# Attention's output turned by VectorE and transfers within SBUF, with statistics, additions and ends put in another order

## The chip, the cores and the metric

One core of a Trainium2 chip runs the kernel. The metric is device time in microseconds (us) for one launch, the median of several runs. Engines: TensorE (PE; its weight loads are PEld), VectorE (DVE), ScalarE (ACT), GpSimd (POOL), SyncE (SP, which here only issues transfers). Each engine works through its own instructions in the order of the program, and engines wait for each other by semaphores.

## The reference, cut to what matters

Two layers over 32 graphs of 512 nodes with 512 features, all float32. `adj` is one 512 x 512 matrix of zeros and ones for all graphs.

```python
q, k, v = (x @ W + b for W, b in ...)                 # 8 heads of 64
scores = einsum('bihd,bjhd->bhij', q, k) / sqrt(64) + where(adj == 0, -1e9, 0)
out = einsum('bhij,bjhd->bihd', softmax(scores), v)   # layer 0: attention
x = layernorm(x + out)
x = layernorm(x + einsum('nm,bmd->bnd', adj, x) @ weight + bias)   # layer 1
```

## The kernel before

One batch `b` is one graph. A tile holds 128 partitions; the 512 rows of `x` lie as four blocks in `X[b]` (names `xs`, in the last batch `xT`). All work is written out by hand in one order (`manual_schedule`), and a batch is a loop step in which the stages of neighbouring batches are laced together: while batch `b` does attention, PE also makes q, k and v of batch `b+1` and layer 1 of batch `b-1`.

Products of 512 x 512 are done in seven block products of 256 x 256 instead of eight (the Winograd form of Strassen's method): `project` for q, k, v and `convolve` for layer 1's second product, each 8 matmul records on PE for one product (L367). The order in `convolve` is 1, 2, 5, 6, 7, 3, 4. Product 1 is copied by ScalarE into `MIX` (L533). VectorE adds products 6 and 7 to `MIX` (L535) and GpSimd adds `MIX` to the blocks x12, and x22 and x21 (L537). VectorE adds the others straight from the bank (L539).

Attention works on heads in pairs (`hp`, 2 x 64 = 128 partitions) and pairs in groups of two (`g`; two groups per batch):

- `scores` (L563): keys x queries into PSUM banks. VectorE takes each bank out with the mask added (L565), ScalarE takes the exponential (L567), GpSimd adds the four exponentials of a pair over the key blocks (L578, `es`).
- `attend` (L587): values x exponentials, so that the output comes as 128 head features x 512 nodes. ScalarE copies it out of its bank into `attT` (L591).
- `fold_squares`: VectorE turns `es` in 32 x 32 squares (L598) and sums (L600); `add_up` has PE finish the sums (L608), VectorE inverts them (`inverse`).
- `residual`: PE turns `attT` back into rows (L619, against the identity), VectorE multiplies by `inverse` (L622) and adds to `X[b]` (L624).

Then come the row statistics (`statistics`, VectorE, L429 and L430), square root and normalisation (ScalarE, L433 and L444), the split of the rows into a high and a low part[...] (`split_high` on ScalarE, L455; `split_low` on VectorE, L459, followed by the bias addition on GpSimd, L460), `aggregate` (L486: adjacency times both parts) and `convolve`.

PSUM has eight banks, handed out in turn by `bank()`: a matmul that needs a bank waits until what was in it eight banks earlier has been taken out. `units_of(b)` lists the interleaved work of a batch in order, and `work_until` runs a share of it at each point:

```python
        for hp in range(g * PAIRS, (g + 1) * PAIRS):
            attend(b, hp)
        folded = folds(b, g)
        ...
        later = scores(*groups[i + 1])
        add_up(b, g)
        ...
        work_until((0.6 if b != B - 2 else 1.0) if g else 0.85)
        for hp in range(g * PAIRS, (g + 1) * PAIRS):
            residual(b, hp)
        work_until(1.0)
```

So PE sees, per batch: attention of group 0, scores of group 1, products of q, k and v, residual, attention of group 1, scores of the next batch's group 0, v's remaining products and `aggregate`, residual, `convolve`. All transfers go through SP's queue: `load_squares` (L248, 16 issues per batch, x in pieces of 128 bytes for the next q, k, v), and `turn_over`: the store of batch `b-2` (L470) and the load of batch `b` (L233) into the same buffer.

After the last batch a tail finishes layer 1 of the last two batches. There `judge` checks that a fast path's conditions held; if not, a general kernel, not run here, would do the work again.

Of the kernel before, what the change touches and what calls it, by code (L numbers as in the profile page):

```python
# [37 lines left out]
FP = mybir.dt.float32  # L38
# [9 lines left out]
P = 128  # L48
HD = 64
# [9 lines left out]
SQ = 32  # L59
# [148 lines left out]
def fast_kernel(ctx: ExitStack, tc, verdict, x, adj, Wq, bq, Wk, bk, Wv, bv, W1, b1, out):  # L208
# [14 lines left out]
    def bank(*shape):  # L223

        return psum.tile([P, *shape], FP, name="bank", tag="bank", bufs=8)
# [56 lines left out]
        nc.gpsimd.tensor_add(fold, fold, ident[:, i * SQ:(i + 1) * SQ])  # L282
    eps = consts.tile([P, 1], FP, name="eps")
    nc.gpsimd.memset(eps, EPS)

    sums = consts.tile([P, NB, GROUP], FP, name="sums")
    inverses = consts.tile([P, NB, GROUP], FP, name="inverses")
# [237 lines left out]
    def convolve(b, i):  # L525

        pm = bank(2, half)
        block_product(pm, YT[b], w1, i)
        x11, x12, x21, x22 = (X[b][:, 2 * r:2 * r + 2, s * half:(s + 1) * half] for r in range(2) for s in range(2))
        if i == 1:  # L530

            MIX[b] = work.tile([P, 2, half], FP, name="mix", tag="q" if b >= B - 3 else "low", bufs=2)
            nc.scalar.activation(MIX[b], pm, AF.Copy)  # L533
        if i in (6, 7):
            nc.vector.tensor_add(MIX[b], pm, MIX[b])  # L535
            for block in (x12,) if i == 6 else (x22, x21):
                nc.gpsimd.tensor_add(block, block, MIX[b])  # L537
        for block in {1: (x11,), 5: (x12, x22), 2: (x11,), 3: (x12,), 4: (x21,)}.get(i, ()):
            nc.vector.tensor_add(block, pm, block)  # L539

    def aggregation(b):

# [4 lines left out]
        return [(convolve, b, i) for i in (1, 2, 5, 6, 7, 3, 4)] if b >= 0 else []  # L547


    E, ES, AT, SQUARES, PART, INVERSE = {}, {}, {}, {}, {}, {}  # L550
    PAIRS = GROUP // 2

    def scores(b, g):
# [26 lines left out]
    def attend(b, hp):  # L580
        po = bank(N)
        for j in range(NB):
            e = E.pop((b, hp, j))
            for s in range(2):
                h = 2 * (hp % 2) + s
                values = V[b][hp // 2][:, j, h * HD:(h + 1) * HD]
                nc.tensor.matmul(po[s * HD:(s + 1) * HD, :], values, e[:, s, :],  # L587
                                 start=(j == 0), stop=(j == NB - 1))
        SQUARES[b, hp] = work.tile([P, 2, N], FP, name="e", bufs=8)
        AT[b, hp] = work.tile([P, N], FP, name="attT")  # L590
        nc.scalar.activation(AT[b, hp], po, AF.Copy)  # L591

    def fold_squares(b, hp):

        if hp % PAIRS == 0:
            PART[b, hp // PAIRS] = work.tile([P, GROUP, N // SQ], FP, name="part", bufs=1)
        square = SQUARES.pop((b, hp))
        nc.vector.transpose(square.rearrange("p s n -> p (s n)"), ES.pop((b, hp)).rearrange("p s n -> p (s n)"))  # L598
        heads = slice(2 * (hp % PAIRS), 2 * (hp % PAIRS) + 2)
        nc.vector.tensor_reduce(PART[b, hp // PAIRS][:, heads, :], square.rearrange("p s (j f) -> p s j f", f=SQ),  # L600
                                axis=AX.X, op=ALU.add)
# [12 lines left out]

    def residual(b, hp):
        at = AT.pop((b, hp))
        pt = bank(NB, 2, HD)
        for c in range(NB):
            nc.tensor.transpose(pt[:, c, :, :], at[:, c * P:(c + 1) * P], ident)  # L619
        first = 2 * hp % GROUP  # L620
        inverse = INVERSE[b, 2 * hp // GROUP][:, :, first:first + 2]
        nc.vector.tensor_mul(pt, pt, inverse[:, :, :, None].to_broadcast([P, NB, 2, HD]))  # L622
        cols = X[b][:, :, hp * P:(hp + 1) * P]
        nc.vector.tensor_add(cols, pt.rearrange("p c s d -> p c (s d)"), cols)  # L624
        if hp == HP - 1 and b < B - 1:
            for c in range(NB):
                statistics(b, 0, c)

# [47 lines left out]
    def weighed(units):  # L676

        weight = {project: 0.5, aggregate: 0.55, x_transpose: 0.13, convolve: 0.5}
        return [(u, weight.get(u[0], 0.0)) for u in units]

    def units_of(b):

        made, turned = projections(b + 1), flips(b + 2)
        splits, gathered = aggregation(b - 1)
        young, old, seen = norm(b - 1, 0) if b < B - 1 else [], norm(b - 1, 1), survey(b - 2)
        ready = [(turn_over, b)] if 1 < b < B - 1 else []
        if b == B - 1:


            older = convolution(b - 2)  # L690
            lows = [(split_low, b - 1, d) for d in range(DB - 1)]
            units = weighed(lows[:2] + older[:3] + lows[2:] + splits[3:] + older[3:5] + older[5:] + gathered + seen)
            return units, [sum(w for _, w in units)] * 2

        if old:
            both = [[(f, b - 1, slice(0, 2 * NB))] for f in (square_root, invert_root)]
            behind = [seen[:2], seen[2:]] + both + [old[2:4], old[4:] + ready] + [[u] for u in young[2:]]
        else:
            behind = [ready] + [[u] for u in young]
        if b == 0:  # L700
            behind = [[]] + [[(sum_weights, w1, n)] for n in range(4)] + [[(look_for_low_half, c)] for c in range(NB)]
        behind += [[] for _ in range(11 - len(behind))] + [splits[:1], [], splits[1:2]]
        behind += [[] for _ in range(16 - len(behind))]
        units = []
        for k, unit in enumerate(made[:16]):
            units += [unit] + behind[k]
        first = sum(w for _, w in weighed(units))
        values = made[16:]
        units += values[:3] + gathered[:1] + splits[2:3] + gathered[1:2] + values[3:] + splits[3:]
        if b == B - 2 > 0:  # L710
            units += [(load, B - 1)]
        units += gathered[2:3] + turned[:1] + gathered[3:]
        convolved = convolution(b - 1) if b < B - 2 else []
        for k in range(7):
            units += convolved[k:k + 1] + (turned[k + 1:k + 2] if k < 3 else turned[4:] if k == 4 else [])
        units = weighed(units)
        return units, [first, sum(w for _, w in units)]

# [2 lines left out]
    for i, (b, g) in enumerate(groups):  # L721
        if g == 0:
            units, ends = units_of(b)
            done = 0.0

        def release():
            run(later)
            later.clear()

        def work_until(part):  # L730

            nonlocal done
            begin = ends[g - 1] if g else 0.0
            while units and (units[0][1] == 0 or done < begin + (ends[g] - begin) * part - 0.3):
                unit, w = units.pop(0)
                run([unit])
                done += w
                if unit[0] == (project if b < B - 1 else convolve):
                    if b == B - 1 or unit[3] == 7:
                        release()  # L740

        for hp in range(g * PAIRS, (g + 1) * PAIRS):
            attend(b, hp)
        folded = folds(b, g)
        if i == len(groups) - 1:
            run(folded)
            add_up(b, g)
            break
        run(folded[:1] + flips(1) + folded[1:] if i == 0 else folded)
        later = scores(*groups[i + 1])  # L750
        add_up(b, g)
        if g == 0 and b + 2 < B:
            load_squares(b + 2)
        work_until((0.6 if b != B - 2 else 1.0) if g else 0.85)
        for hp in range(g * PAIRS, (g + 1) * PAIRS):
            residual(b, hp)
        work_until(1.0)
        if g == GROUPS - 1:
            run([u for u, _ in units])
            if b == B - 2:  # L760
                run(norm(b, 0) + [(split_high, b, d) for d in range(DB - 1)])
        release()
# [17 lines left out]
    run(rest[3 + NB:])  # L780
    for c in range(NB):
        add_bias(t, c)
    run(seen[:2])
    aggregate_rows(t)


# [6 lines left out]
        nc.vector.bn_stats(halves[c][:, s, :], X[t][:, c, s * half:(s + 1) * half])  # L793

    old = norm(t, 1)
    beside = {1: seen[2:], 2: old[:2], 5: old[2:3], 6: old[3:5], 7: old[5:]}
    for unit in last:
        run([unit] + beside.get(unit[2], []))
        if unit[2] == 2:
            well = judge()  # L800
        if unit[2] == 7 and t > 0:
            store(t - 1)
        for c, s in {2: ((0, 0), (1, 0)), 3: ((2, 1), (3, 1), (0, 1), (1, 1)), 4: ((2, 0), (3, 0))}.get(unit[2], ()):
            half_statistics(c, s)
            if (c < 2) == (s == 1):
                if t + 1 not in STAT:
                    for table, name, shape in ((STAT, "stat", (2 * NB, 2)), (RSTD, "rstd", (2 * NB,)),
                                               (SHIFT, "shift", (2 * NB,))):
                        table[t + 1] = work.tile([P, *shape], FP, name=name, bufs=3)
                nc.vector.bn_aggr(STAT[t + 1][:, NB + c, :], halves[c])  # L810
# [35 lines left out]
```

## Time and profile before

| | |
|---|---|
| time, median of 3 runs | 2858.62 us (2857.77 to 2861.34) |
| span of the profile | 2858.2 us |
| PE busy | 2820.5 us (99%) |
| VectorE busy | 2086.4 us (73%) |
| GpSimd busy | 1746.2 us (61%) |
| ScalarE busy | 1146.6 us (40%) |
| granted TensorE clock | 0.996 |
| DMA, mean | 38 GB/s |

A share of busy time is an average over the whole span. The chain of work that ended last follows the waits back from the last instruction, and names at each moment the instruction that the end hung on. Columns in a row of the chain are start, length and what ran; in a row of the timeline start, length, engine, line, operation, output and inputs, and in brackets the idle time before it with what ended it. PE's rows count matmul records, of which one matmul instruction of this float32 kernel leaves two (the turning of `attT` and L486 leave one).

### The profile page before, as it was taken

To read this page: it belongs to the slowest core of one execution; us is meant where nothing else is said; L and a number is where in the kernel's file an instruction comes from. 1 tells how busy PE (TensorE), PEld (TensorE's weight loads), DVE (VectorE), ACT (ScalarE), POOL (GpSimd) and SP (SyncE) were. 2 spreads that over 40 slices of the span, in tenths; PEclk is the share of its full clock that TensorE was granted. 3 is DMA by queue.
4 is the path that set the end of the run, shared out by engine and by line. 5 is a ranking of instruction groups with operands and counts; after the bars stand their busy time and mean duration, and the time that the engine had idled before them with its cause. 6 is when DMAs were issued, how large, how long until landed. Compare 5 with 4: busy or idle time off the path is not lost.

```text
span 2858.2 us, 35612 instructions
## 1 busy us (share of the span) xinstructions
PE 2820.5 (99%) x13346; PEld 1983.1 (69%) x13346; DVE 2086.4 (73%) x3415; ACT 1146.6 (40%) x1550; POOL 1746.2 (61%) x1096
## 2 busy tenths in 40 slices
PE   8999999999999999999999999999999999999997
PEld 6676776766767767667677676676676766766765
DVE  6767777677776777777777767777677777777786
ACT  3344343343433443434434334343344342443443
POOL 4565665665756656656566656575665665665763
PEclk9999999999999999999999999999999999999998
DMA  5001111111101111011111111110111111111001
GB/s 154 12 8 41 45 30 30 41 34 45 45 16 45 34 41 45 16 45 34 41 45 35 25 42 33 45 45 15 45 34 41 45 24 36 36 39 45 30 16 45
DMA packets 302577, 108.81 MB, mean 38 GB/s; under 512 B 264256, under 2 KB 268352, under 8 KB 302400
## 3 DMA queue, kind: packets, MB, share of 16 engines
q1 hardware_dynamic: 302400, 106.47, 14.6%
q8 instruction: 108, 1.77, 0.3%
q14 instruction: 69, 0.57, 0.1%
HBM read 72.88 MB, written 33.55 MB: 37 GB/s over the span
## 4 chain that ended last, share of the span: by engine, by line
PE 96%; DVE 2%; POOL 1%; SPq 0%; issue 0%; ACT 0%; DMA 0%; DVEq 0%; ACTq 0%; POOLq 0%
PE bank L367 53%; PE bank L563 17%; PE bank L587 15%; PE bank L486 8%; PE bank L619 2%; PE bank L608 0%; POOL es L578 0%; DVE bnst L429 0%; SPq L253 0%; DMA xin<-in_x_dram 0%; DVE e L598 0%; POOL xs L460 0%; DVE bank L622 0%; POOL xs L537 0%; DVE part L600 0%
## 5 line engine op out<-in xcount | busy, mean ns | idle before, releaser
L565 DVE SCALAR_TENSOR_TENSOR e<-gap,bank 128x512 f32<-128x512 uint8 x1024 | 617.4, 678 | 65.0 <-PE bank L563 65.0
L578 POOL TENSOR_TENSOR es<-e 128x1024 f32<-128x1024 f32 x128 | 316.2, 2470 | 530.5 <-ACT e L567 530.5
L578 POOL TENSOR_TENSOR es<-es,e 128x1024 f32<-128x1024 f32 x256 | 618.7, 2417 | 20.1
L567 ACT ACTIVATE e<-e 128x1024 f32<-128x1024 f32 x512 | 524.2, 1052 | 130.8 <-DVE e L565 103.0
L591 ACT ACTIVATE attT<-bank 128x512 f32<-128x512 f32 x128 | 76.4, 598 | 1046.7 <-PE bank L587 1046.7
L563 PE MATMUL bank<-q,k 64*128 64x512 f32 x2048 | 488.4, 603 | 2.4 <-ACT attT L591 2.4
L587 PE MATMUL bank<-e,v 128*64 128x512 f32 x2048 | 453.8, 595 | 1.9 <-DVE v L402 1.9
L367 PE MATMUL bank<-wv,xT 128*128 128x256 f32 x1792 | 411.5, 381 | 3.1 <-DVE q L402 3.1
L563 PEld LDWEIGHTS bank<-q,k 64*128 64x128 f32 x2048 | 223.7, 186 | 265.6 <-issue 161.2
L367 PE MATMUL bank<-xT,wk 128*128 128x256 f32 x1792 | 404.0, 380 | 0.7 <-DVE wk L317 0.7
L367 PE MATMUL bank<-xT,wq 128*128 128x256 f32 x1792 | 401.0, 381 | 2.5 <-DVE wq L317 1.8
L367 PE MATMUL bank<-w,yT 128*128 128x256 f32 x1792 | 394.0, 380 | 1.6 <-DVE yT L518 1.6
L367 PEld LDWEIGHTS bank<-xT,wk 128*128 128x128 f32 x1792 | 341.1, 190 | 47.6 <-PE bank L367 1.1
L367 PEld LDWEIGHTS bank<-w,yT 128*128 128x128 f32 x1792 | 339.2, 191 | 47.2 <-DVE yT L518 2.0
L367 PEld LDWEIGHTS bank<-xT,wq 128*128 128x128 f32 x1792 | 337.7, 190 | 49.2 <-POOL xT L331 1.8
L367 PEld LDWEIGHTS bank<-wv,xT 128*128 128x128 f32 x1792 | 335.3, 190 | 49.3 <-issue 3.4
L587 PEld LDWEIGHTS bank<-e,v 128*64 128x64 f32 x2048 | 141.6, 137 | 278.8 <-issue 268.2
L537 POOL TENSOR_TENSOR xs<-xs,mix 128x512 f32<-128x512 f32 x93 | 117.6, 1279 | 204.2 <-DVE mix L535 204.2
L460 POOL TENSOR_TENSOR xs<-xs,b_r 128x512 f32<-128x512 f32 x124 | 157.2, 1278 | 114.4 <-DVE low L459 114.4
L402 DVE TENSOR_TENSOR q<-bank,q 128x512 f32<-128x512 f32 x96 | 66.4, 691 | 183.0 <-PE bank L367 157.2
L444 ACT ACTIVATE xs<-xs,shift,rstd 128x512 f32<-128x512 f32 x248 | 184.8, 811 | 29.8 <-DVE shift L439 29.8
L489 ACT ACTIVATE yT<-bank 128x512 f32<-128x512 f32 x124 | 74.3, 599 | 294.9 <-PE bank L486 294.9
(115 smaller groups left out, 3016.7 us busy)
## 6 DMA issues: line engine op xcount, KB each, us to landing
xin<-in_x_dram SPq DMA_DIRECT2D x496, 64.0 KB, 2.3
xs<-in_x_dram SPq DMA_DIRECT2D x31, 1024.0 KB, 5.1
out_dram<-xs SPq DMA_DIRECT2D x31, 1024.0 KB, 4.3
xin<-in_x_dram SPq DMA_DIRECT2D x4, 256.0 KB, 3.6
wq<-in_L_gnn_Wq_dram SPq DMA_DIRECT2D x2, 512.0 KB, 6.5
wk<-in_L_gnn_Wk_dram SPq DMA_DIRECT2D x2, 512.0 KB, 8.2
yT<-in_adj_dram SPq DMA_DIRECT2D x1, 1024.0 KB, 7.8
wv<-in_L_gnn_Wv_dram SPq DMA_DIRECT2D x2, 512.0 KB, 8.8
```

What stands on the lines that cost most here:

```text
L367: nc.tensor.matmul(pm[:, r, :], left[:, d, r * P:(r + 1) * P], right[:, d, :], start=(d == 0), stop=(d == 1))
L444: nc.scalar.activation(row, row, AF.Identity, bias=SHIFT[t][:, slot:slot + 1], scale=RSTD[t][:, slot:slot + 1])
L460: nc.gpsimd.tensor_add(cols, cols, b1_r[:, None, d * P:(d + 1) * P].to_broadcast([P, NB, P]))
L486: nc.tensor.matmul(pm.rearrange("p a n -> p (a n)"), part, adjT[:, n % NB, :], start=(n == 0), stop=(n == 2 * NB - 1))
L489: nc.scalar.activation(yt[:, d // 2:d // 2 + 3:2, d % 2, :], pm, AF.Copy)
L537: nc.gpsimd.tensor_add(block, block, MIX[b])
L563: nc.tensor.matmul(ps[s], keys[:, j * P:(j + 1) * P], queries, start=True, stop=True)
L565: nc.vector.scalar_tensor_tensor(e[:, s, :], gap[:, j, :], NEG * root, ps[s], op0=ALU.mult, op1=ALU.add)
L567: nc.scalar.activation(e, e, AF.Exp, scale=1.0 / root)
L578: nc.gpsimd.tensor_add(ES[b, hp], ES[b, hp] if j > 1 else E[b, hp, 0], E[b, hp, j])
L587: nc.tensor.matmul(po[s * HD:(s + 1) * HD, :], values, e[:, s, :], start=(j == 0), stop=(j == NB - 1))
L591: nc.scalar.activation(AT[b, hp], po, AF.Copy)
```

## The change

Attention's output is no longer turned by PE. In the new `turn_out`, VectorE transposes the PSUM bank in 32 x 32 squares into `attT` (which also empties the bank, in place of ScalarE's copy), and 16 transfers per pair, SBUF to SBUF, carry the squares to their place in a new tile `rows`. `residual` then has ScalarE scale 8 pieces of 128 x 64 by `inverse`, each with its own scalar per partition, and GpSimd adds the result to `X[b]`. This frees PE and VectorE of their part. In the last two batches' second groups the old way stays.

The rest is order. The folds stand between the two `attend` calls' output steps, `statistics` of layer 0 go from `residual` to the next batch's projections, the square roots of the two layers are taken apart, the addition of `MIX` to x21 comes after product 4 instead of before it, the look for low halves in batch 0 moves later, the last group's folds run early, and the tail's statistics change order.

```diff
@@ convolve
         if i in (6, 7):
             nc.vector.tensor_add(MIX[b], pm, MIX[b])
-            for block in (x12,) if i == 6 else (x22, x21):
+            for block in (x12,) if i == 6 else (x21, x22) if b == B - 1 else (x22,):
                 nc.gpsimd.tensor_add(block, block, MIX[b])
         for block in {1: (x11,), 5: (x12, x22), 2: (x11,), 3: (x12,), 4: (x21,)}.get(i, ()):
             nc.vector.tensor_add(block, pm, block)
+        if i == 4 and b < B - 1:
+            nc.gpsimd.tensor_add(x21, x21, MIX[b])
@@ attend
-        SQUARES[b, hp] = work.tile([P, 2, N], FP, name="e", bufs=8)
-        AT[b, hp] = work.tile([P, N], FP, name="attT")
-        nc.scalar.activation(AT[b, hp], po, AF.Copy)
+        ...
+        OUT[b, hp] = po
+
+    def turn_out(b, hp):
+        po = OUT.pop((b, hp))
+        at = AT[b, hp] = work.tile([P, N], FP, name="attT")
+        if b >= B - 2 and hp >= PAIRS:
+            nc.scalar.activation(at, po, AF.Copy)
+            return
+        nc.vector.transpose(at, po)
+        turned = at.rearrange("p (c j f) -> p c j f", c=NB, j=P // SQ)
+        rows = ROWS[b, hp] = work.tile([P, NB, P], FP, name="rows")
+        for i in range(P // SQ):
+            for j in range(P // SQ):
+                nc.sync.dma_start(rows[j * SQ:(j + 1) * SQ, :, i * SQ:(i + 1) * SQ],
+                                  turned[i * SQ:(i + 1) * SQ, :, j, :])
@@ residual
+        if (b, hp) in ROWS:
+            rows = ROWS.pop((b, hp))
+            for c in range(NB):
+                for s in range(2):
+                    part = rows[:, c, s * HD:(s + 1) * HD]
+                    nc.scalar.activation(part, part, AF.Identity, bias=zero, scale=inverse[:, c, s:s + 1])
+            nc.gpsimd.tensor_add(cols, cols, rows)
+        else:
...
-        if hp == HP - 1 and b < B - 1:
+        if hp == HP - 1 and b == B - 2:
             for c in range(NB):
                 statistics(b, 0, c)
@@ units_of
-            units = weighed(lows[:2] + older[:3] + lows[2:] + splits[3:] + older[3:5] + older[5:] + gathered + seen)
+            last = folds(b, 1)
+            units = weighed(older[:3] + last[:1] + lows[2:] + splits[3:] + older[3:] + gathered + last[1:] + seen)
...
+        fresh = [(statistics, b - 1, 0, c) for c in range(NB)] if young else []
         if old:
-            both = [[(f, b - 1, slice(0, 2 * NB))] for f in (square_root, invert_root)]
-            behind = [seen[:2], seen[2:]] + both + [old[2:4], old[4:] + ready] + [[u] for u in young[2:]]
+            behind = [seen[:2], seen[2:], old[:2], old[2:4] + fresh[:2], old[4:] + ready + fresh[2:]] + [
+                [u] for u in young]
...
-            units += convolved[k:k + 1] + (turned[k + 1:k + 2] if k < 3 else turned[4:] if k == 4 else [])
+            units += convolved[k:k + 1] + (turned[k + 1:k + 2] if k < 3 else turned[4:] if k == 6 else [])
@@ the loop over groups
         for hp in range(g * PAIRS, (g + 1) * PAIRS):
             attend(b, hp)
-        folded = folds(b, g)
+            if i < len(groups) - 1:
+                fold_squares(b, hp)
+            turn_out(b, hp)
+            if hp == 0:
+                run(flips(1) if i == 0 else [(split_low, b - 1, d) for d in range(2)] if i == len(groups) - 2 else [])
...
-        work_until((0.6 if b != B - 2 else 1.0) if g else 0.85)
+        work_until(0.6 if g else 0.85)
@@ the tail
-        for c, s in {2: ((0, 0), (1, 0)), 3: ((2, 1), (3, 1), (0, 1), (1, 1)), 4: ((2, 0), (3, 0))}.get(unit[2], ()):
+        for c, s in {2: ((0, 0), (1, 0)), 3: ((0, 1), (1, 1)), 4: ((2, 1), (3, 1), (2, 0), (3, 0))}.get(unit[2], ()):
```

## The prediction

> **What bounds the kernel now.** I read the page's busy line first, then the chain that ended last in order of time for one batch from the middle, then the waits, then the same stretch engine by engine.
>
> ```profile
> PE 2820.5 (99%) x13346; PEld 1983.1 (69%) x13346; DVE 2086.4 (73%) x3415; ACT 1146.6 (40%) x1550; POOL 1746.2 (61%) x1096
> ...
> PE 96%; DVE 2%; POOL 1%; SPq 0%; issue 0%; ACT 0%; DMA 0%; DVEq 0%; ACTq 0%; POOLq 0%
> ```
>
> PE is busy 99% of the span and carries 96% of the chain. A busy PE isn't PE at its peak, so the chain has to say where PE works and where it only seems to. One batch, from the chain in order of time (start, length, what):
>
> ```profile
> 1010.08 7.02 PE bank L587 x32
> 1017.09 8.01 PE bank L563 x32
> 1025.10 0.19 PE bank L608 x8
> 1025.29 22.64 PE bank L367 x104
> 1047.93 0.87 PE bank L619 x8
> 1048.81 5.18 PE bank L367 x24
> 1053.99 7.02 PE bank L587 x32
> 1061.01 7.14 PE bank L563 x32
> ...
> 1084.93 0.87 PE bank L619 x8
> 1085.81 12.09 PE bank L367 x56
> 1097.90 0.57 PE bank L587
> ```
>
> The period is 1097.90 - 1010.08 = 87.82 us. Two things stand out: the transposes L619 (attention's output) stand alone on PE for 0.87 us twice a batch, and the same 32 score matmuls take 8.01 us after the first group and 7.14 after the second. VectorE in that stretch explains the 0.87 us of difference:
>
> ```profile
> 1013.64 0.69 DVE L539 TENSOR_TENSOR xs<-bank,xs 128x512 f32<-128x512 f32 x1 [2.03 <-POOL xs L537]
> 1014.25 1.23 DVE L598 STREAM_TRANSPOSE e<-es 128x1024 f32<-128x1024 f32 x1
> 1015.52 1.22 DVE L600 TENSOR_REDUCE part<-e 128x32 f32<-128x1024 f32 x1
> 1016.65 1.24 DVE L598 STREAM_TRANSPOSE e<-es 128x1024 f32<-128x1024 f32 x1
> 1017.93 1.22 DVE L600 TENSOR_REDUCE part<-e 128x32 f32<-128x1024 f32 x1
> 1019.06 9.64 DVE L565 SCALAR_TENSOR_TENSOR e<-gap,bank 128x512 f32<-128x512 uint8 x16
> ```
>
> The last convolution add waits for GpSimd, the folds follow, and the first score leaves its bank at 1019.06, 1.97 us after PE began the scores; in the second group it is 1062.10 - 1061.01 = 1.09 us. PE runs out of banks. So PE is the limit, and each us taken off it counts while the other engines keep up.
>
> **What the Trainium skill says.** (1) VectorE: DVE Perf Modes, The three transpose paths: VectorE gives "a 4×4 grid of independently-transposed 32×32 blocks, not one 128×128 transpose". That is why the changed kernel needs 16 transfers per pair of heads. The trace has this operation only from SBUF (L351, 695 ns for 128x512). (2) ScalarE: Activation LUTs, What ACT_TABLE_LOAD costs: 186 ns + 0.833 ns per element, 93 ns per pointer operand, and neighbours overlap by 93 ns. The trace agrees: L444, 512 elements and two pointers, takes 811 ns against 799 by the formula. (3) DMA: Bandwidth & Descriptors, Why small descriptors are slow (HBM only): transfers within SBUF don't pay for 128-byte pieces as those to HBM do. No run here shows one. (4) SBUF — State Buffer, Who interferes with whom: a VectorE instruction with two SBUF inputs blocks against a GpSimd one that reads SBUF. The trace fits: L459 (two SBUF inputs) averages 1049 ns, L539 (one) 668.
>
> **The change, part by part.**
>
> PE. The transposes go for all pairs but the four of the last two batches' second groups: 31 x 2 = 62 groups x 0.87 us (the chain's row) = 53.9 us, all on the path. Nothing is added to PE.
>
> VectorE. L622 and L624 go (688 + 692 ns) and one transpose of the output comes: bounds 598 ns (ScalarE's copy out of the same bank) and 800, I take 0.70. Net -0.68 us per pair, and 4 x 0.68 = 2.7 us less per batch of 64.24 busy. The statistics (4 x 0.84) move from just before the convolution to the next batch's projections, where VectorE waited for PE (4.56 us before the second L402 of q alone). So VectorE reaches the convolution without the 6.2 us of work that held it from 1085.94 to 1091.93, and evicts it as PE goes. The addition of MIX to x21 goes behind the eviction of product 4, so the last eviction no longer waits for GpSimd (2.03 us). By hand, from the start of attention S: last eviction ends S+0.7, fold of the first pair S+3.2, transposed output (PE ready S+3.8) S+4.5, second fold S+7.0, second output (PE ready at S+7.3) S+8.0, first score out S+8.1, which is as early as in the second group. The 0.87 us goes: 30 batches x 0.87 = 26; I take 0.8 each, 24 us.
>
> A new wait is that of VectorE for PE in the middle of attention. Behind it stand the second fold and then the score evictions; by the times above it ends 3 us before PE wants the first bank.
>
> ScalarE. L591 goes (598 ns), 8 scalings of 128x64 come per pair. No row has this form; its bounds are 0.30 us (L433, 128x8 with a pointer) and 0.43 us (186 + 2 x 93 + 53, the skill). In a row I take 0.33 each: 16 x 0.33 = 5.3 us per group. In the first group ScalarE idles from 1042.85 to 1057.62, 14.8 us, and hides it. In the second it stands between the last yT copy (ends 1085.6) and MIX (L533): MIX comes at about 1091 instead of 1087.6, while VectorE wants it for product 6, which PE ends at about 1091.7. Just hidden. Busy total: 1147 - 74 + 992 x 0.33 to 0.43, at most 1500 us, 54%.
>
> GpSimd. One addition of 128x512 more per pair: 124 x 1.28 (L460) = 159 us, 1905 in all, 69%. Its row is unbroken from 1066.83 to 1091.1; the new additions follow that, end near 1094, and the x12 addition, which in before began at 1096.84, comes after them. Hidden.
>
> DMA. 64 issues per batch more. Bounds for one: 0.39 us (a 1 MB load's issue) and 0.53 (16 of L248's 512 pieces back to back). 16 x 0.5 = 8 us a pair, 16 us a group, and 2.3 us to land: the first pair's begin at S+4.5, so the second pair's rows lie there at S+23, 16 us after attention's end. ScalarE wants them 24 us (second group) or 31 us (first) after it. All 64, and L248's 16, fill about 40 us of the queue's 85. Store and load of x stand behind them and come about 1 us later than at 1038.15 and 1044.13; x's reader is now GpSimd, idle in before from 1054.3 to 1066.8. Hidden.
>
> Start. In batch 0 PE stood still from 95.55 to 99.12 (the look for low halves before an eviction) and from about 126 to 134, in part, behind residual and statistics. With the first moved and the second off VectorE: 3 + 6.5 = 9.5 us.
>
> End. The last fold is done early, and PE's wait of 4.3 us for it (L608 <- L600) goes; two subtractions before the scores and two additions of GpSimd cost some of it. I take -3, between -7 and +5.
>
> Sum: 53.9 + 24 + 9.5 + 3 = 90.4. 2858.6 - 90.4 = 2768.
>
> **The rivals.** A, a part is given back (17 in 100): MIX, ScalarE's 5.3 us or GpSimd's longer row holds up the end of each convolution, the scores' 0.87 us stays, and about 0.3 us a batch more is lost. For it: MIX's margin is under 1 us, and the forecast hangs on timings by hand. Against: eight banks cover several us. Time: 2858.6 - 53.9 - 12.5 + 31 x 0.3 = 2802.
>
> B, slower (6 in 100): the transfers are the bound. The queue holds 64 issues, 16 loads (8.5 us) and about 8 us of store and load per batch; it passes 85 us when one issue takes over 1.07. At 1.2 us a batch takes 93 us, and 31 x (93 - 87.8) + 2858.6 is about 3020. Against: twice the dearest issue of the trace, with a quarter of its pieces.
>
> C, it goes better (3 in 100): PE's other small stalls (22.64 + 5.18 us for 128 matmuls where the pace of 12.09 for 56 makes 27.63) vanish too, and the ends give 7: 2750.
>
> **How the numbers follow.** The forecast has 74 in 100. The range goes from 2752 (the ends at their best, and most of C) to 2804 (A, or the start and end at their worst). That leaves out B, C and the edges, about 15 in 100. Faster: the forecast, A and C, less 2 for A's far edge, 0.92; within 0.2%: 0.02; slower: 0.06.
>
> **What would show it.** Right: L619 falls from 512 to 16 matmuls; the chain stays over 95% PE; the batch's period is 85.2 us; both score rows are 7.1; VectorE's transposes of the output last 0.7; ScalarE's scalings 0.3 to 0.43; the queue issues at 0.5 us or less. Wrong: waits of VectorE for MIX, of ScalarE for rows, or of PE for a bank in each batch, or a period above 86.

## The result, and the profile after

| runs side by side | before | after |
|---|---|---|
| time, median | 2859.65 us (2857.77 to 2861.34) | 2787.62 us (2786.90 to 2789.08) |
| ratio, 95% interval | 1 | 0.9749 (0.9732 to 0.9766) |
| span of the profile | 2858.2 us | 2785.0 us |
| a batch in the middle, from attention to attention | 87.82 us | 85.49 us |

The change saves 72 us. The busy line of the page after, and its row for the transfers' queue (packets, MB, share of 16 engines):

```profile
PE 2752.0 (99%) x12850; PEld 1917.2 (69%) x12850; DVE 2033.2 (73%) x3349; ACT 1406.0 (50%) x2447; POOL 1898.1 (68%) x1221
...
q1 hardware_dynamic: 588096, 139.10, 22.8%
```

PE has 496 matmul records fewer (62 groups x 8, the transposes) and is still busy 99%. ScalarE and GpSimd took over work and are far from full. The chain that ended last can't be followed beyond the last part of this span, so I read the middle from the timelines. PE, from one attention of the second group to the same in the next batch (columns start, length, engine, line, operation):

```profile
1031.61 7.09 PE L592 MATMUL bank<-e,v 128*64 128x512 f32 x32
1038.63 7.21 PE L568 MATMUL bank<-q,k 64*128 64x512 f32 x32
...
1061.52 1.09 PE L488 MATMUL bank<-adjT,high 128*128 128x512 f32 x4
1062.45 12.25 PE L369 MATMUL bank<-w,yT 128*128 128x256 f32 x56
1074.63 7.09 PE L592 MATMUL bank<-e,v 128*64 128x512 f32 x32
1081.65 7.51 PE L568 MATMUL bank<-q,k 64*128 64x512 f32 x32
...
1117.10 3.22 PE L592 MATMUL bank<-e,v 128*64 128x512 f32 x14
```

1117.10 - 1031.61 = 85.49 us. No transpose stands between `aggregate` (L488) and the convolution (L369). But the two score rows aren't alike yet: 7.51 us against 7.21, where before has 8.07 against 7.21 in this view (8.01 against 7.14 in the chain's rows). VectorE over the convolution and that attention (in brackets: idle time before, and what ended it):

```profile
1063.28 0.42 DVE L493 TENSOR_TENSOR yT<-bank,yT 128x256 f32<-128x256 f32 x1 [1.12 <-ACT yT L491]
1069.06 0.69 DVE L541 TENSOR_TENSOR xs<-bank,xs 128x512 f32<-128x512 f32 x1 [5.35 <-ACT mix L535]
...
1075.30 0.69 DVE L537 TENSOR_TENSOR mix<-bank,mix 128x512 f32<-128x512 f32 x1 [1.38 <-POOL xs L539]
1075.91 1.28 DVE L541 TENSOR_TENSOR xs<-bank,xs 128x512 f32<-128x512 f32 x2
1077.11 1.24 DVE L623 STREAM_TRANSPOSE e<-es 128x1024 f32<-128x1024 f32 x1
...
1079.51 0.70 DVE L606 STREAM_TRANSPOSE attT<-bank 128x512 f32<-128x512 f32 x1
...
1083.15 9.62 DVE L570 SCALAR_TENSOR_TENSOR e<-gap,bank 128x512 f32<-128x512 uint8 x16
```

The first eviction of the convolution, product 1 added to x11 (L541), waits 5.35 us for ScalarE's copy of the same product into `MIX` (L535). The evictions of the other products bunch behind it, the last ends at 1077.19, 2.56 us after attention began, and the first score leaves its bank 1.50 us after PE began the scores. ScalarE shows why the copy is late:

```profile
1062.65 0.60 ACT L491 ACTIVATE yT<-bank 128x512 f32<-128x512 f32 x1 [1.56 <-PE bank L488]
1063.15 5.40 ACT L650 ACTIVATE rows<-rows,zero,inverse 128x64 f32<-128x64 f32 x16
1068.44 0.58 ACT L535 ACTIVATE mix<-bank 128x512 f32<-128x512 f32 x1
```

The residual's 16 scalings stand ahead of it in ScalarE's order. The other part that missed is the start. Where batch 0's step goes over into batch 1's, VectorE and PE show:

```profile
120.89 0.88 DVE L310 TENSOR_TENSOR attT<-yT,high 128x512 f32<-128x512 f32 x1
121.81 0.69 DVE L311 TENSOR_REDUCE inexact<-attT 128x1 f32<-128x512 f32 x1
127.04 1.14 DVE L310 TENSOR_TENSOR attT<-yT,high 128x512 f32<-128x512 f32 x1 [4.54 <-DMA rows<-attT]
...
135.66 1.20 DVE L623 STREAM_TRANSPOSE e<-es 128x1024 f32<-128x1024 f32 x1
```

```profile
123.63 1.94 PE L592 MATMUL bank<-e,v 128*64 128x512 f32 x8
130.24 6.75 PE L592 MATMUL bank<-e,v 128*64 128x512 f32 x24 [4.67 <-DVE v L404]
136.92 3.70 PE L568 MATMUL bank<-q,k 64*128 64x512 f32 x14
141.80 6.57 PE L568 MATMUL bank<-q,k 64*128 64x512 f32 x18 [1.19 <-DVE attT L606]
```

The look for low halves (L310, L311) writes its scratch into a buffer of the tag `attT`, which the transfers of `rows` still read. Behind the waiting look stand v's evictions, and behind those PE's attention of batch 1. The step from batch 1's first attention to batch 2's is 95.71 us; before has 89.50, and later batches of the change take 85.5.

By stage of the span: up to batch 2's first attention 219.7 us before and 219.3 after; from there to batch 30's 2458.8 and 2394.2; to the end 179.7 and 171.5. So nearly all of the gain came in the steady batches (64.6) and the end (8.2), and 0.4 in the start.

### The profile page after: what moved, and what is told of

It reads as the page before. It is cut to its first block, busy times and chain, and to the rows that moved or that the text cites. A ratio compares the mean times of both kernels' runs of the same rounds, so it can differ in the third digit from the quotient of the medians.

```text
span 2785.0 us, 39215 instructions
## 1 busy us (share of the span) xinstructions
PE 2752.0 (99%) x12850; PEld 1917.2 (69%) x12850; DVE 2033.2 (73%) x3349; ACT 1406.0 (50%) x2447; POOL 1898.1 (68%) x1221
## 5 line engine op out<-in xcount | busy, mean ns | idle before, releaser
L568 PE MATMUL bank<-q,k 64*128 64x512 f32 x2048 | 477.3, 601 | 1.5 <-DVE attT L606 1.5
L369 PE MATMUL bank<-wv,xT 128*128 128x256 f32 x1792 | 405.4, 381 | 0.0
L369 PE MATMUL bank<-xT,wk 128*128 128x256 f32 x1792 | 403.0, 379 | 0.7 <-DVE wk L319 0.7
L369 PE MATMUL bank<-xT,wq 128*128 128x256 f32 x1792 | 401.0, 381 | 2.5 <-DVE wq L319 1.7
L568 PEld LDWEIGHTS bank<-q,k 64*128 64x128 f32 x2048 | 212.9, 187 | 264.3 <-issue 141.4
L369 PE MATMUL bank<-w,yT 128*128 128x256 f32 x1792 | 392.3, 379 | 0.5 <-DVE yT L520 0.5
L369 PEld LDWEIGHTS bank<-w,yT 128*128 128x128 f32 x1792 | 340.0, 190 | 48.1 <-DVE yT L520 0.9
L369 PEld LDWEIGHTS bank<-xT,wk 128*128 128x128 f32 x1792 | 340.2, 190 | 47.2 <-PE bank L369 1.1
L369 PEld LDWEIGHTS bank<-xT,wq 128*128 128x128 f32 x1792 | 337.7, 190 | 49.1 <-POOL xT L333 1.8
L369 PEld LDWEIGHTS bank<-wv,xT 128*128 128x128 f32 x1792 | 337.5, 190 | 47.4 <-DVE e L570 0.8
L650 ACT ACTIVATE rows<-rows,zero,inverse 128x64 f32<-128x64 f32 x992 | 335.0, 428 | 3.5 <-DMA rows<-attT 3.4
L651 POOL TENSOR_TENSOR xs<-xs,rows 128x512 f32<-128x512 f32 x122 | 154.5, 1288 | 195.0 <-DMA xs<-in_x_dram 195.0
L541 DVE TENSOR_TENSOR xs<-bank,xs 128x512 f32<-128x512 f32 x186 | 120.1, 672 | 157.1 <-ACT mix L535 156.9
```

The lines of the kernel that those rows point to most:

```text
L369: nc.tensor.matmul(pm[:, r, :], left[:, d, r * P:(r + 1) * P], right[:, d, :], start=(d == 0), stop=(d == 1))
L568: nc.tensor.matmul(ps[s], keys[:, j * P:(j + 1) * P], queries, start=True, stop=True)
L650: nc.scalar.activation(part, part, AF.Identity, bias=zero, scale=inverse[:, c, s:s + 1])
L651: nc.gpsimd.tensor_add(cols, cols, rows)
```

## The experiments

Theory: two things hold back what the change could give, and they are separate. In each batch product 1's addition waits for a copy that stands behind the scalings; at the end of batch 0's step VectorE is late for PE because of the look. Rivals: GpSimd's or the statistics' place sets the convolution's end; the queue of transfers costs the time.

**Product 1 added before it is copied.** In `convolve`:

```diff
         if i == 1:
+            nc.vector.tensor_add(x11, pm, x11)
             nc.scalar.activation(MIX[b], pm, AF.Copy)
...
-        for block in {1: (x11,), 5: (x12, x22), 2: (x11,), 3: (x12,), 4: (x21,)}.get(i, ()):
+        for block in {5: (x12, x22), 2: (x11,), 3: (x12,), 4: (x21,)}.get(i, ()):
```

> For product 1 of the convolution VectorE's addition to x11 is put ahead of ScalarE's copy into MIX; nothing else moves. Theory R (two readers of one bank are ordered, and VectorE stands behind a copy that stands behind 16 scalings): VectorE's 5.35 us of waiting before the first convolution addition goes, the 32 score matmuls after group 0 fall from 7.51 to about 7.14 us, the period from 85.49 to 85.1, the time by 30 x 0.37 = 11 us to about 2776. Theory G (GpSimd's additions of MIX hold the convolution's end anyway): the scores stay at 7.5 and the time at 2787.

2781.16 us (ratio to before 0.9729, 0.9715 to 0.9742), a batch 85.21, both score rows at 7.2. VectorE's timeline of this version:

```profile
1060.68 0.42 DVE L493 TENSOR_TENSOR yT<-bank,yT 128x256 f32<-128x256 f32 x1 [1.14 <-ACT yT L491]
1061.78 0.69 DVE L535 TENSOR_TENSOR xs<-bank,xs 128x512 f32<-128x512 f32 x1 [0.67 <-PE bank L369]
```

The addition (L535 here) follows PE after 0.67 us, and the period falls by 0.28 us. Both engines read product 1's bank, and the program has the one wait for the other. Of that the Trainium skill says (PSUM — Partial Sum Buffer, PSUM bank collisions raise a hardware error) that the compiler's scheduler adds a dependency between any two instructions on different engines that touch the same bank and the same 32 partitions of it, reads and writes alike, ScalarE against VectorE too. The trace agrees: VectorE waits 5.35 us for a ScalarE instruction whose output it doesn't use, and the wait is gone when their order is exchanged.

**The copy before the scalings.** In batches 1 to 29 the share of the work list run before the second group's `residual` goes up, so that product 1 and its copy come first:

```diff
-        work_until(0.6 if g else 0.85)
+        work_until((0.65 if 0 < b < B - 2 else 0.6) if g else 0.85)
```

> Product 1 of the convolution, and with it ScalarE's copy into MIX, is put ahead of the 16 scalings of the second group (batches 1 to 29); the order of the two readers of the bank stays. Theory R: as good as the other edit, about 2776, because the copy then comes at once. A third theory S (ScalarE's 5.4 us of scalings harm wherever they stand, since what comes behind them is late): no gain, about 2787, with a wait for ScalarE at another place of the batch.

2779.69 us (0.972, 0.9707 to 0.9733), a batch 85.21, both score rows 7.21. ScalarE still does as many scalings and GpSimd as many additions, and the period is the same as with the first edit: what costs the 0.28 us is the order of copy and scalings, not their length.

**The look's scratch in another buffer** (tag `low` instead of `attT`), alone and with the first edit:

> The look for low halves in batch 0 takes its scratch tile from the buffers of low in place of those of attT. If PE's 4.67 us and 1.19 us of standing still in batch 0 come from VectorE waiting for the row transfers to leave attT: both go, the time falls by about 5 us to 2782. If they come from VectorE's amount of work there: no change, 2787.

2789.36 us (0.9756, 0.9743 to 0.9769): no gain. VectorE of this version:

```profile
124.52 1.28 DVE L404 TENSOR_TENSOR v<-bank,v 128x512 f32<-128x512 f32 x2
130.31 1.21 DVE L310 TENSOR_TENSOR low<-yT,high 128x512 f32<-128x512 f32 x1 [4.52 <-ACT high L308]
```

The wait for a transfer is gone, v's evictions end 4 us sooner, and the look then waits 4.52 us for ScalarE's copies (L308), which stand behind scalings that wait 3.43 us for rows. PE loses 5.29 and 0.93 us in the scores instead of 4.67 and 1.19 in attention and scores: the wait moved.

> The addition ahead of the copy and the look's scratch tile elsewhere, together. If the two causes are apart, the gains add: 11 + 5 us, about 2771, near the 2768 that was forecast. If they overlap, less.

2783.17 us (0.9734, 0.9721 to 0.9747), a miss by 12 us: only the first edit shows in it.

**One transfer per pair instead of 16.** The squares aren't put in their places, so that part of the computation is left out; bytes and waits stay.

```diff
-        for i in range(P // SQ):
-            for j in range(P // SQ):
-                nc.sync.dma_start(rows[j * SQ:(j + 1) * SQ, :, i * SQ:(i + 1) * SQ],
-                                  turned[i * SQ:(i + 1) * SQ, :, j, :])
+        nc.sync.dma_start(rows, at.rearrange("p (c f) -> p c f", c=NB))
```

> One transfer of the whole tile in place of 16 per pair: the squares don't get to their places, so the part of the computation that puts them in order is left out. If the queue's 64 issues per batch (0.6 us each) cost nothing but in batch 0: 2787 less some 6 us for batch 0, about 2781, and the same period of 85.5. If late loads of x or late rows hold the steady batches: a shorter period, 2770 or less.

2787.13 us (0.9749, 0.9734 to 0.9763), the period 85.49 as before the edit: the queue's 64 issues cost nothing in the steady batches. The start didn't gain the 6 us that I had expected either, though here no engine waits for rows between 100 and 160 us. VectorE:

```profile
126.67 2.32 DVE L310 TENSOR_TENSOR attT<-yT,high 128x512 f32<-128x512 f32 x1 [0.98 <-ACT high L308]
...
129.63 2.12 DVE L310 TENSOR_TENSOR attT<-yT,high 128x512 f32<-128x512 f32 x1
...
134.79 1.20 DVE L620 STREAM_TRANSPOSE e<-es 128x1024 f32<-128x1024 f32 x1
```

The folds begin at 134.79 instead of 135.66. So late rows are only what shows last in the change; with them on time, the look itself, from 121.21 to 132.47 with v's evictions in it and partly behind ScalarE's copies, keeps the folds nearly as late. Its comparisons (L310) are also slow there: the last two take 2.32 and 2.12 us while GpSimd adds exponentials, where before had 0.68 or 0.69 for each, with GpSimd idle. My theory of the start was too narrow: the place of the look has to go, not one of its waits.

**The look earlier.** The first edit, and the look back in batch 0's first half of projections, where before had it, but with scratch `low`. In before its scratch in `attT` had made VectorE wait there for PE's transposes, which read `attT`:

```profile
95.64 0.69 DVE L308 TENSOR_TENSOR attT<-yT,high 128x512 f32<-128x512 f32 x1 [13.03 <-PE bank L619]
```

The edit:

```diff
-            behind = [[]] + [[(sum_weights, w1, n)] for n in range(4)]
+            behind = [[]] + [[(sum_weights, w1, n)] for n in range(4)] + [[(look_for_low_half, c)] for c in range(NB)]
...
-        looked = [(look_for_low_half, c) for c in range(NB)] if b == 0 else []
+        looked = []
```

> The addition ahead of the copy (as in the first run), and the look for low halves taken back to the first group's projections of batch 0 with its scratch tile in low's buffers. The look alone out of attT gave nothing: VectorE then waited 4.52 us for ScalarE's copy for the look, which stood behind scalings that waited for row transfers. If that is the whole cause of the start's loss (the step from batch 1's first attention to batch 2's takes 95.1 us against 85.2 later), VectorE and PE no longer wait for row transfers in batch 0, the step falls to about 86, and the time by up to 9 us to about 2772. If the late rows of batch 0's second group hold PE in another way: no gain, 2781.

2772.07 us (0.9693, 0.9679 to 0.9706), faster than both kernels. VectorE, then PE:

```profile
124.65 2.48 DVE L353 STREAM_TRANSPOSE xT<-xin 128x512 f32<-128x512 f32 x4
127.06 1.20 DVE L624 STREAM_TRANSPOSE e<-es 128x1024 f32<-128x1024 f32 x1
```

```profile
123.88 7.09 PE L593 MATMUL bank<-e,v 128*64 128x512 f32 x32
130.90 8.23 PE L569 MATMUL bank<-q,k 64*128 64x512 f32 x32
```

The folds begin 8.6 us sooner, PE's attention is unbroken, and the step to batch 2 is 86.22 us instead of 95.71. So the look is what the start's loss hangs on. At this place only the buffer `low` was tried.

**Everything but the turning.** `turn_out` always has ScalarE copy, and PE transposes for all pairs, as before the change; the order of the changed kernel stays.

```diff
-        if b >= B - 2 and hp >= PAIRS:
+        if True:
```

> All pairs keep the old way (ScalarE's copy, PE's transposes, VectorE's multiplication and addition); the change's order stays. Theory N (the order is worth what it saves by itself): the scores after group 0 fall from 8.01 to about 7.14 us, 30 x 0.87 = 26 us, time about 2833. Theory D (it needs the turn, since VectorE still does 2.75 us of multiplying and adding just before the convolution): scores at 7.5 us, about 2845. Either way the 54 us of transposes stay.

2826.56 us (0.9886, 0.9871 to 0.9902): the order alone saves 33 us. A batch takes 86.96 us, 0.86 less than before, both score rows last 7.21, and VectorE doesn't wait for `MIX`'s copy. The turning takes the period from 86.96 to 85.49, 1.47 us, and to 85.21 with product 1's addition first, 1.75 us, as two transposes of 0.87 make. The start says something too: with no transfers of rows at all, the step from batch 1's first attention to batch 2's is still 93.52 us, 6.6 more than this version's period. Late rows aren't needed for the start's loss.

**The statistics back behind the residual**, the rest as in the changed kernel:

```diff
-        if hp == HP - 1 and b == B - 2:
+        if hp == HP - 1 and b < B - 1:
...
-        fresh = [(statistics, b - 1, 0, c) for c in range(NB)] if young else []
+        fresh = []
```

> The statistics of layer 0 go back to just behind the residual; the turn and the rest of the order stay. VectorE then waits for GpSimd's addition of rows, which ends 8.8 us after the convolution's start, before it may empty the convolution's banks, and has 3.4 us of statistics to do first. Theory: evictions 5.5 us later than now, the scores after group 0 longer by about 5.9 us, 30 x 5.9 = 176 us, about 2960, slower than before the change. Rival: eight banks cover the delay, under 2800.

2985.94 us (1.0439, 1.0423 to 1.0455), slower than before. VectorE, and then PE:

```profile
1146.05 0.69 DVE L431 BATCH_NORM_STATS2 bnst<-xs 128x6 f32<-128x512 f32 x1 [7.54 <-POOL xs L651]
...
1156.09 1.28 DVE L541 TENSOR_TENSOR xs<-bank,xs 128x512 f32<-128x512 f32 x2
```

```profile
1149.44 7.09 PE L592 MATMUL bank<-e,v 128*64 128x512 f32 x32
1156.45 2.85 PE L568 MATMUL bank<-q,k 64*128 64x512 f32 x12
1160.45 1.12 PE L568 MATMUL bank<-q,k 64*128 64x512 f32 x2 [1.15 <-DVE attT L606]
1163.46 7.17 PE L568 MATMUL bank<-q,k 64*128 64x512 f32 x18 [1.88 <-DVE attT L606]
```

The statistics wait for GpSimd's addition of rows, all evictions of the convolution stand behind them, and the scores take 1170.63 - 1156.45 = 14.2 us. In this order the turning pays only with the statistics out of the way: the two halves of the change belong together.

**MIX's addition to x21 before product 4 again**, on top of the 2772.07 us version:

```diff
-            for block in (x12,) if i == 6 else (x21, x22) if b == B - 1 else (x22,):
+            for block in (x12,) if i == 6 else (x22, x21):
...
-        if i == 4 and b < B - 1:
-            nc.gpsimd.tensor_add(x21, x21, MIX[b])
```

> This is the version with product 1's addition first and the look moved (2772.07 us), with one part of the change undone: the addition of MIX to x21 stands before product 4 again. If that part is needed, VectorE's eviction of product 4 waits for GpSimd's two additions (2 x 1.28 us after MIX's last sum), about 1 us; the folds, the transposed outputs and the first score come that much later, the scores after group 0 last about 8.0 us instead of 7.21, the period is about 86.0 and the time 2772 + 30 x 0.8 = 2796. If the place of the statistics alone removed the scores' stall, the scores stay at 7.2, the period at 85.21 and the time at 2772.

2770.93 us (0.9692, 0.9676 to 0.9708): no loss, and my expectation of 2796 fails. VectorE, and then PE:

```profile
1064.63 0.69 DVE L542 TENSOR_TENSOR xs<-bank,xs 128x512 f32<-128x512 f32 x1 [2.02 <-POOL xs L540]
```

```profile
1063.44 7.09 PE L590 MATMUL bank<-e,v 128*64 128x512 f32 x32
1070.46 7.21 PE L566 MATMUL bank<-q,k 64*128 64x512 f32 x32
```

The wait of 2.02 us for GpSimd is back and costs nothing, since the eviction still ends 1.9 us after attention's start. The runs together give how late it may be (one batch of the middle each):

| version | last eviction ends, after attention's start | first score leaves its bank, after PE began the scores | scores |
|---|---|---|---|
| look earlier | 0.8 us | 1.2 us | 7.21 us |
| order only | 0.8 us | 1.2 us | 7.21 us |
| x21 back | 1.9 us | 1.2 us | 7.21 us |
| the change | 2.6 us | 1.5 us | 7.51 us |
| before | 4.3 us | 2.0 us | 8.07 us |
| statistics back | 7.9 us | 6.9 us | 14.2 us |

The order between last eviction and first score isn't the same in all of them (in before only the two folds stand there, in the change two turned outputs as well), so the third column compares better: each us that the first score comes later costs PE about one. In the changed kernel's order the last eviction may come about 2 us after attention's start for nothing.

**Twice as many transfers**, each half as large (two blocks of columns instead of four):

> Each of the 16 transfers of a pair is split in two by column blocks, so that the queue has 128 issues of rows per batch instead of 64, with the same bytes. If an issue costs the queue the same 0.64 us whatever its size, 128 x 0.64 = 82 us, the 16 loads' 8.6 and the store and load's about 1 make 91 us or more, over the period of 85.5: the queue becomes the bound, the period is 91 to 95 us and the time about 2787.6 + 30 x 5.5 to 30 x 9.5 = 2950 to 3070. If the issue's cost follows the number of pieces (half as many: about 0.35 us), all stays hidden and the time is 2787 to 2790, the period 85.5.

3792.61 us (1.3263, 1.3241 to 1.3285), far beyond what I had expected. Rows of the queue's `rows` issues, first of the change, then of this version (count: shortest, median and longest in ns):

```profile
L611 SPq DMA_DIRECT2D rows<-attT x1984: 585/599/1993, 61.2 to 2719.0; - x199
```

```profile
L612 SPq DMA_DIRECT2D rows<-attT x3968: 585/595/1893, 61.6 to 3732.6; - x199
```

An issue costs the same with half the pieces. 128 of them at 0.595 us and a gap of 0.05 make 83 us, the loads 8.6; but a batch takes 118.7 us, from 1508.89, where the queue begins the loads, to 1627.57. Of the rest, 14 us a batch are a ring of waits, which the trace shows and no run takes apart. ScalarE and PE of this version:

```profile
1570.91 2.42 ACT L651 ACTIVATE rows<-rows,zero,inverse 128x64 f32<-128x64 f32 x7 [10.07 <-DMA rows<-attT]
1573.24 0.57 ACT L535 ACTIVATE mix<-bank 128x512 f32<-128x512 f32 x1
```

```profile
1574.59 4.98 PE L592 MATMUL bank<-e,v 128*64 128x512 f32 x16 [11.32 <-DVE xs L541]
```

Scalings wait for rows, the copy into `MIX` stands behind the scalings, product 1's addition waits for the copy, PE's attention waits for the addition's bank, and the queue waits for the output of that attention (453 us in 32 waits, about 14 us each). The copy and the addition in this ring are those that cost the change 0.28 us.

**Both misses removed the other way**: copy before the scalings, look earlier.

> The other way to remove the two misses together: product 1 and its copy before the residual's scalings (instead of the addition before the copy), and the look for low halves moved to the first group's projections. If the two causes are separate, their gains add: 2779.7 (copy first alone) less about 10 (what moving the look gave on top of the addition first) = 2770, period 85.2. If they overlap, about 2779.

2770.17 us (0.9686, 0.967 to 0.9702), a batch 85.20. The causes are separate. The intervals of the three versions near 2771 overlap, so none is shown to be the best.

## Why the prediction was right, and where it was off

The forecast was 2768 us and the time is 2787.62, faster by 72 where 90.4 were summed. Direction and main cause hold, and the range holds the time; two terms were mis-sized. By stage, the sum had 13.0 us for the start (9.5, and the transposes of four groups), 71 for the 28 batches that follow (1.74 and 0.8 each) and about 6 for the end. The traces have 0.4, 64.6 and 8.2. So most of what is missing is missing in the start.

- Transposes, 53.9 us: right. 496 of 512 records are gone, and with the copy's wait removed the turning is worth 1.75 us a batch, as the sum had it. In the changed kernel 1.47 arrive.
- The scores' stall, 0.8 us a batch: the order alone gives 0.86, which also shows in equal score rows of 7.21. In the change itself the row falls only from 8.07 to 7.51. The step that failed is "Just hidden" for `MIX`. For the reader that it named it holds: the copy ends at 1068.44 + 0.58 = 1069.02, and product 6, the fourth, is there at about 1062.45 + 4 x 12.25 / 7 = 1069.45. But another reader of the same bank comes first: product 1's own addition to x11 is ordered behind the copy and could have begun nearly 5 us sooner. In the trace of before that wait is covered, since VectorE was late with statistics anyway. So the first sign that the prediction had named for being wrong, a wait of VectorE for `MIX`, stands in each batch. The cost is 85.49 - 85.21 = 0.28 us a batch, some 8 us; the two edits that remove it gain 6.5 and 7.9. With both misses removed the timetable made by hand comes true: last eviction at 0.8 us after attention's start, first score out at 8.2, where it had 0.7 and 8.1.
- Which part of the order does it: the forecast put it on the statistics and on x21 together. With product 1's addition first, x21's place is free. That leaves the statistics, 3.4 us of VectorE's work just before the evictions, but no run separates them from the new place of the folds.
- Start, 9.5 us: the second term that failed, in two ways. The first part of it, 3 us, came: PE reaches batch 0's second attention at 100.45 instead of 106.15, 5.7 us sooner, of which 0.8 were there at the first attention already and 0.87 are transposes. The other part, 6.5 us, was misread. It was taken from a stretch of the chain that VectorE holds (125.98 to 134.00). But where another engine holds the chain, PE may still be at work. PE's own rows of before:

```profile
126.65 3.62 PE L367 MATMUL bank<-wv,xT 128*128 128x256 f32 x16
130.20 1.94 PE L587 MATMUL bank<-e,v 128*64 128x512 f32 x8
134.00 5.37 PE L587 MATMUL bank<-e,v 128*64 128x512 f32 x24 [1.86 <-DVE v L402]
139.30 7.69 PE L563 MATMUL bank<-q,k 64*128 64x512 f32 x32
```

Between these rows PE lost 1.86 us, and 0.5 in the scores (7.69 against 7.21), so only about 2.4 were to be had. And the work that left VectorE's queue was replaced: the change puts the look just there, with its waits for rows and for ScalarE behind the scalings. I had counted what left in batch 0 and not what came. Moving the look gives 9.5 us in that step and 9.1 in the time. That this is the number of the term is chance: the step of before, 89.50, holds no look, and 86.22 is only 3.3 us less, 1.74 of them transposes.

- End: 8.2 us, where about 6 were summed. PE's waits in it add up to 11.2 us before and 4.7 after, and the wait of 4.29 for the last fold is gone.
- Scalings: 0.338 us each in a row (5.40 / 16), taken 0.33. One by itself lasts 428 ns on average. The Trainium skill (ScalarE: Activation LUTs, What ACT_TABLE_LOAD costs) gives 186 + 53 + 2 x 93 = 425 and, less 93 for neighbours, 332; the trace agrees with both within 2%.
- VectorE's transposes of the output, 0.71 us on average, 0.70 taken: right. GpSimd at 1898 us, 1905 forecast, and its waits for x and rows hidden: right.
- Transfers: an issue took 0.60 us and a gap of 0.05, over the upper bound of 0.53 taken from a transfer with four times the pieces. Hidden all the same, as one transfer per pair shows. For rival B the arithmetic was too kind: it let a batch lose only what the queue's work exceeds the period by, 6 us with 128 issues (83 + 8.6 - 85.5), and that run lost 33 (118.7 - 85.5).
- Of the rivals, A had the mechanism (`MIX` held up by ScalarE's scalings) and about its size, 0.3 us a batch; it was wrong that the whole 0.87 us of the scores would stay. The time lies between it and the forecast. With both misses removed it is 2770 to 2772, near the 2768 of the forecast. That is partly luck: in the version with the look earlier the start gains 9.6 us of 13.0, the middle 73.2 where 71 were summed, and the end 4.5 of 6.

## What to carry to other kernels

When work moves to an idle engine, list what stands behind it in that engine's order and find every instruction that waits for those, also the ones that only read the same bank: a wait that was covered before the change comes out when its reader gets early. Reckon a late hand-over by its slack, not by its length (here the last eviction could come about 2 us after attention's start for nothing, and later cost PE time). Before counting a stretch of the chain as another engine's stall, read that engine's own rows. And count for each engine and stage what arrives there, not only what leaves; the start of a pipeline isn't a shorter copy of its middle.

## What I had not expected of the hardware

Issues of 16 KB within SBUF (128 pieces of 128 bytes) follow each other at 0.64 us (10 in 6.39). That is slower than the loads of x, 64 KB in 512 pieces, at 0.53 (16 in 8.55), and halving them to 64 pieces leaves the issue itself at 0.595. The data land 1.8 us after the issue in both.

In these runs PE's clock falls where PE pauses. With PE busy 99% the granted clock is 0.996 to 0.998, with the statistics back 0.962, with twice the transfers 0.891. After the pause of 11.32 us in that version, 16 attention matmuls take 4.98 us where 16 without a pause take 3.65, at a clock of 0.75 over the next 5.4 us. The Trainium skill tells of this (TensorE: Matmul & The Clock Gate, Part 1: The HAM clock gate): an idle window takes the clock down until PE has been busy again. The trace agrees, and so a stall costs more than its own length: the 118.7 us a batch hold slower matmuls as well as waits.
